# Reordering the opening of a Perceiver kernel: key rows in rounds, zeros moved, key and centre loads in another order

## The chip, the cores and the metric

The kernel runs on one core of a Trainium2 chip. The metric is the device time of one execution in microseconds (us); lower is better. A core has the engines PE (TensorE, matrix products), DVE (VectorE), ACT (ScalarE) and POOL (GpSimd), each with its own in-order stream of instructions, and SP (SyncE), whose stream here holds nearly all DMA issues, also in order. Engines wait for each other through semaphores.

## The reference

The whole computation is a Perceiver block of three residual parts on `x` (16 batches x 32 channels x 512 points):

```
x = x + xattn(ctx, layernorm(x), ...)    # graph features: what this change touches
x = x + attn(layernorm(x), ...)          # a Mamba-2 style scan
x = x + ffn(layernorm(x), ...)           # low-rank SwiGLU feed-forward
```

What matters is how the first part begins. Three channels of the context are taken as coordinates of the 512 points of each batch. They are quantized to 10 bits, four keys are made of them (two Morton, two Hilbert), and the points are sorted by each key:

```
keys = [morton(q), morton(qt), hilbert(q), hilbert(qt)]      # qt: x and y exchanged
inds = [window(argsort(k)) for k in keys]                    # 10 neighbours in sorted order
```

Then two graph layers follow. Each takes for every point and each of the four orders the 10 neighbours' features minus the point's own (the centre), does a small attention over the 10, a linear map and a 1x1 convolution, an instance norm, a leaky ReLU and a maximum over the neighbours. The third convolution joins the layers' outputs.

## The kernel before, in words

Four batches of 32 channels fill the 128 partitions: a "group". Four groups by two layers make eight stages, run in an order written out by hand in `graph_part`: `order = [(0, 0), (1, 0), (0, 1), ...]`. A stage has 43 blocks of 12 points. A software pipeline runs over all 8 x 43 blocks: in each step `scores`, `greatest`, `expo`, `sums`, `shares`, `turn`, `mapped`, `outputs` and `reduce` work on blocks up to four apart, and `differences` (POOL, L756 to L767) makes neighbour minus centre six blocks ahead (`LEAD`). After every third block, `differences` also issues four DMAs that copy its tile `DD` into the block-diagonal tile `DX` (L777). The other parts of `DX` have to be zero, and the scores (L809, PE) read `DX`.

The sort is done by counting. `compare` (L536) puts one product on PE that gives, for 128 points against all 512, the differences of their keys, and one ACT instruction (L537, `sgn`) that adds up their signs: this is the rank. A key is cut into bf16 rows in DRAM (`own` and `others`), and `load_keys` (L530, L531) brings the rows of one batch and one method by two DMAs to `kl` and `kr`, of which there are two sets. `rank_step` does one comparison per call, in order. The first 64 (`FIRST`) are batches 0 to 3 by methods 0 and 1 (eight each, `HALF`), then batches 0 to 3 by methods 2 and 3, the Hilbert keys.

`node_orders` makes the keys on DVE, in a generator that is stepped by hand. Its helper `rows` transposes a key on PE (L278) and splits it into bf16 rows: copy a part (L287; on ACT for the Morton key, on DVE for the Hilbert key), subtract it on PE (L289), copy the next part. Then it stores the rows (L293, L294). Before, all of the Hilbert key's `rows` stand between comparisons 24 and 25 in PE's order. After comparison 31 ACT writes zeros into the three `DX` tiles (L593).

`prep` prepares a stage, one piece per step. For the first stage it runs ahead of the loop, one `rank_step` after each piece. For layer 0 it does a layer norm (through ACT at L71 and L73), stores the features to DRAM (`dC`, L631), transposes them (`pf` L635, `FT` L637 on ACT) and splits them. Then, for each of the group's four batches: one-hot rows from the ranks (`oh`, DVE, L720), a product with the features on PE (`place`, L689, `pp`) that puts them in sorted order, a copy by ACT (`so`, L696, two buffers), a store to DRAM (`dS`, L700) and, three ticks later, four loads in another layout (`fs`, L706). The centre features come from `dC` by 16 loads (`crep`, L667). When all is there, DVE copies the last column (L738), and `differences` may begin.

`prep` queues stores and loads in a list `later` of delays, counted down by `tick`. Before, the 16 centre loads are one entry of that list: with delay 18 in the first stage, with delay 1 (at once) in the others. In the first stage they are issued behind the first batch's `fs` loads, and the 8 key loads of batch 4 follow them on SP, ahead of the store of the second batch.

Of the kernel before, what the change touches and what calls it, by code (L numbers as in the profile page):

```python
# [8 lines left out]
F32 = mybir.dt.float32  # L9
# [9 lines left out]
P = 128  # L19
# [4 lines left out]
M = 4  # L24
# [163 lines left out]
def node_orders(nc, pool, tmp, ps, X, idx, id32, nid, own, others):  # L188
# [81 lines left out]
    def rows(keys, j, copy):  # L270

        R = 2 * B
        at = slice(R * j, R * j + R)
        made = []
        for nm, src in zip("hl", keys):
            pr = ps.tile([R, D], F32, tag="pr", name=f"pr{nm}{j}", bufs=2)
            for c in range(4):
                nc.tensor.matmul(  # L278
                    pr[:, c * P:(c + 1) * P], lhsT=src[:, c].rearrange("p m b -> p (m b)"), rhs=id32,
                    is_transpose=True, start=(c == 0), stop=True, skip_group_check=True,  # L280
                )
            made.append((pr, pool.tile([R, 3, D], BF16, name=f"r{nm}{j}")))
        for k in range(3):
            for (pr, t), n, r0 in zip(made, (2, 3), (0, 4)):
                if k >= n:
                    continue
                copy(t[:, k], pr)  # L287
                if k < n - 1:
                    nc.tensor.matmul(  # L289
                        pr, lhsT=nid[:R, :R], rhs=t[:, k], start=False, stop=True, skip_group_check=True  # L290
                    )
                    continue
                nc.sync.dma_start(out=others[at, r0:r0 + n], in_=t[:, :n])  # L293
                nc.sync.dma_start(out=own[at, r0 + n:r0 + 2 * n], in_=t[:, :n])  # L294
# [3 lines left out]
    key = pool.tile([P, 2, N], I32, name="key0")  # L298
# [4 lines left out]
    for j in range(2):  # L303
        nc.vector.scalar_tensor_tensor(
            key[:, j], S[:, j], 2, key[:, j], ALU.logical_shift_left, ALU.bitwise_or
        )
    rows(parts(key.rearrange("p j n -> p (j n)"), 0), 0, nc.scalar.copy)
    yield

    H = [pool.tile([P, 2, N], I32, name=f"H{i}") for i in range(3)]  # L310
# [4 lines left out]
    flat = [h.rearrange("p a n -> p (a n)") for h in H]  # L315
# [39 lines left out]
    for s in (1, 2, 4, 8):  # L355
        t = new("y")
# [11 lines left out]
    nc.vector.scalar_tensor_tensor(key, XX[:, 0], 2, key, ALU.logical_shift_left, ALU.bitwise_or)  # L368
    keys = parts(key, 1)
    yield  # L370
    rows(keys, 1, nc.vector.tensor_copy)


def graph_part(nc, tc, cx, I, dram, id32, ones, xt, F0, layernorm_steps, rstd_steps, scan_input):
# [172 lines left out]
    def rank_step(tile_of):  # L547

        n = ranked[0]
        if n == 4 * M * B:  # L550
            return
        ranked[0] += 1
        if n < FIRST:
            half, k = divmod(n, HALF)
            b, c, m = half % 4, k // 2, 2 * (half // 4) + k % 2
        else:
            b, k = divmod(n, 4 * M)
            c, m = divmod(k, M)
        if n == 0:
            load_keys(0, (0, 1))  # L560
        compare(tile_of(n), b, c, m)
        if n < FIRST:
            if k == 1 and half < 7:
                load_keys((half + 1) % 4, (0, 1) if half < 3 else (2, 3))
            elif k == 1:
                load_keys(4, range(M))
        elif k == 4 and b + 1 < B:
            load_keys(b + 1, range(M))

# [12 lines left out]
    def first_tile(n):  # L582
        return kps.tile([P, D], F32, tag="kd", name=f"kd{n}", bufs=3)

    for n in range(3 * HALF + 1):
        rank_step(first_tile)
    for _ in orders:
        pass
    while ranked[0] < 4 * HALF:
        rank_step(first_tile)  # L590
    for t in DX:
        flat = t.rearrange("p h b q -> p (h b q)").bitcast(F32)
        nc.scalar.mul(flat, ones[:, 0:1].to_broadcast([P, flat.shape[-1]]), 0.0)  # L593


    id30 = gc.tile([P, QB], F32, name="id30")
# [22 lines left out]
    def later_tile(n):  # L619
        return ps_1.tile([P, D], F32, tag="misc", bufs=2, name=f"kd{n}")  # L620

    def prep(g, layer, delay=1):


        L, co, npair, WA, WC, HB = layers[layer]
        key = f"{L}_{g}"
        src = F1[g] if layer else F0[:, g]
        if layer == 0:
            yield from layernorm_steps(sm, src, xt[:, g], f"g{g}")
        dC = dram.tile([P, D], F32, name=f"dC{key}")  # L630
        nc.sync.dma_start(out=dC, in_=src)  # L631

        pf = ps_1.tile([P, 4, P], F32, tag="misc", bufs=2, name=f"pf{key}")
        for c in range(4):
            nc.tensor.transpose(pf[:, c], src[:, c * P:(c + 1) * P], id32)  # L635
        FT = wk.tile([P, 4, P], F32, tag="FT", name=f"FT{key}", bufs=1)
        nc.scalar.copy(FT, pf)  # L637
        yield

        F3 = [wk.tile([P, 4, P], BF16, tag=f"F3_{k}", name=f"F3_{k}{key}", bufs=1) for k in range(3)]  # L640
        for k in range(3):
            nc.vector.tensor_copy(F3[k], FT)
            if k < 2:
                nc.vector.tensor_tensor(FT, FT, F3[k], ALU.subtract)
                yield

        c16 = wk.tile([P, D], F16, tag="c16", name=f"c16{key}", bufs=1)
        nc.vector.tensor_copy(c16, src)
        yield
        c32 = wk.tile([P, D], F32, tag="c32", name=f"c32{key}", bufs=1)  # L650
        nc.vector.tensor_copy(c32, c16)
        yield
        hc = wk.tile([P, npair, D], F32, tag="hc", name=f"hc{key}")
        for pr in range(npair):
            ph = ps_1.tile([P, D], F32, tag="misc", bufs=2, name=f"ph{key}_{pr}")
            nc.tensor.matmul(ph, lhsT=WC[:, pr], rhs=c32, start=True, stop=True)
            nc.scalar.activation(hc[:, pr], ph, AF.Identity, bias=HB)
            yield

        crep = big.tile([P, 4, D], F32, tag="crep", name=f"crep{key}", bufs=2)  # L660
        later = []

        def copies():
            for b in range(4):
                for m in range(M):
                    r = 32 * b + 8 * m
                    nc.sync.dma_start(  # L667
                        out=crep[r:r + 8], in_=dC[32 * b:32 * b + 32].rearrange("(h c) n -> c h n", h=4)
                    )

        later.append([delay, copies])

        def tick():
            for t in list(later):
                t[0] -= 1
                if t[0] <= 0:
                    later.remove(t)
                    t[1]()

        yield  # L680

        fs = big.tile([P, 4, D + 4], F32, tag="fs", name=f"fs{key}", bufs=2)
        pend = []

        def place():
            b, c, ohs, pp = pend.pop()
            for m, oh in ohs:
                for k in range(3):
                    nc.tensor.matmul(  # L689
                        pp[32 * m:32 * m + 32, :], lhsT=F3[k][:, c, 32 * b:32 * b + 32], rhs=oh,  # L690
                        start=(c == 0 and k == 0), stop=(c == 3 and k == 2),
                    )
            if c < 3:
                return
            so = wk.tile([P, D], F32, tag="so", name=f"so{key}_{b}", bufs=2)
            nc.scalar.copy(so, pp)  # L696
            dS = dram.tile([P, D], F32, name=f"dS{key}_{b}")

            def store():
                nc.sync.dma_start(out=dS, in_=so)  # L700
                later.append([3, spread])

            def spread():
                for m in range(M):
                    r = 32 * b + 8 * m
                    nc.sync.dma_start(  # L706
                        out=fs[r:r + 8, :, :D], in_=dS[32 * m:32 * m + 32].rearrange("(h c) n -> c h n", h=4)
                    )

            later.append([2, store])  # L710

        for b in range(4):
            while ranked[0] < ranks_of(4 * g + b):
                yield False
            pp = None
            for c in range(4):
                ohs = []
                for m in range(M):
                    oh = wk.tile([P, D], BF16, tag="oh", name=f"oh{key}_{b}_{m}_{c}", bufs=8)
                    nc.vector.tensor_scalar(  # L720
                        oh, it2, rank[:, c, m, 4 * g + b:4 * g + b + 1], None, ALU.is_equal
                    )
                    ohs.append((m, oh))
                    if m == 1:
                        tick()
                        yield
                if pend:
                    place()
                if c == 0:
                    pp = ps_1.tile([P, D], F32, tag="pp", name=f"pp{key}_{b}")  # L730
                pend.append((b, c, ohs, pp))
                tick()
                yield
        place()
        while later:
            tick()
            yield
        nc.vector.tensor_copy(fs[:, :, D:], fs[:, :, D - 1:D].to_broadcast([P, 4, 4]))  # L738
        made[key] = (fs, crep, hc)
# [214 lines left out]
    made = {}  # L954
    order = [(0, 0), (1, 0), (0, 1), (1, 1), (2, 0), (3, 0), (2, 1), (3, 1)]
    keys = [f"{layers[layer][0]}_{g}" for g, layer in order]
    first = prep(*order[0], 18)
    next(first)
    for _ in first:
        if ranked[0] < FIRST:  # L960
            rank_step(early_tile)
    for gi in range(LEAD):
        differences(0, gi)

# [435 lines left out]
```

## Time and profile before

| what | us |
|---|---|
| median of 3 runs | 2449.3 (2441.37 to 2454.86) |
| the profiled execution | 2442.78 |
| its span, first to last instruction | 2440.9 |
| opening, up to the third batch's `so` copy | 98.62 |
| from there to the first scores of the loop (L809) | 30.36 |
| block loop of the eight stages, from there to about 1400 | 1271 |
| scan and feed-forward parts, the rest | about 1040 |

The profile is of one execution. A row of the timeline gives start, busy time, engine (SPq is the DMA-issuing queue of SP), line, operation, output<-inputs, shape, count, and in brackets the idle time of that engine just before with what ended it. Lines of the waits give the total, the number and the longest. A row of a window gives, for a stretch, each engine's busy time with its number of instructions, the granted PE clock as a share of full speed, the busy share of the DMA engines and GB/s. Line numbers are those of the kernel before.

### The profile page before, as it was taken

To read this page: it belongs to the slowest core of one execution; us is meant where nothing else is said; L and a number is where in the kernel's file an instruction comes from. 1 tells how busy PE (TensorE), PEld (TensorE's weight loads), DVE (VectorE), ACT (ScalarE), POOL (GpSimd) and SP (SyncE) were. 2 spreads that over 40 slices of the span, in tenths; PEclk is the share of its full clock that TensorE was granted. 3 is DMA by queue.
4 is the path that set the end of the run, shared out by engine and by line. 5 is a ranking of instruction groups with operands and counts; after the bars stand their busy time and mean duration, and the time that the engine had idled before them with its cause. 6 is when DMAs were issued, how large, how long until landed. Compare 5 with 4: busy or idle time off the path is not lost. (4 is left out here: it accounts for less than half of the span.)

```text
span 2440.9 us, 88578 instructions
## 1 busy us (share of the span) xinstructions
PE 2135.6 (87%) x39025; PEld 1247.9 (51%) x39146; DVE 1739.5 (71%) x3718; ACT 1098.7 (45%) x2023; POOL 830.9 (34%) x897
## 2 busy tenths in 40 slices
PE   5479677999899677879998879999999999999979
PEld 2145455667667454566777634444444444444422
DVE  8379798888899889988999866653554626455643
ACT  5567556666665334454555322332333424333331
POOL 2056556445446556564655400020211202021200
PEclk9889999999999899999999889999999999999989
DMA  2232232221122233322211222213122131310000
GB/s 48 60 65 65 57 74 61 58 59 44 43 62 59 52 73 65 72 52 67 58 34 40 63 73 75 75 31 95 52 61 65 39 86 31 87 57 22 26 35 17
DMA packets 121624, 137.98 MB, mean 57 GB/s; under 512 B 18398, under 2 KB 79506, under 8 KB 121154
## 3 DMA queue, kind: packets, MB, share of 16 engines
q1 hardware_dynamic: 121240, 132.32, 21.6%
q8 instruction: 307, 5.03, 0.9%
q14 instruction: 77, 0.63, 0.1%
HBM read 77.02 MB, written 12.85 MB: 37 GB/s over the span
## 5 line engine op out<-in xcount | busy, mean ns | idle before, releaser
L846 POOL TENSOR_TENSOR EN<-e,rz 128x480 f32<-128x480 f32 x344 | 342.3, 995 | 561.4 <-DVE rz L844 424.1
L871 PE MATMUL u<-WA,DD 128*32 128x128 bf16 (+1 forms) x16512 | 421.6, 251 | 51.1 <-issue 34.2
L871 PEld LDWEIGHTS <-DD 128*32 128x32 f16 x16512 | 341.1, 99 | 69.8 <-issue 66.0
L876 ACT COPY us<-u 128x512 f32<-128x512 f32 x516 | 301.9, 586 | 151.9 <-PE u L871 133.6
L831 ACT ACTIVATE e<-s,smc 128x480 f32<-128x480 f32 x344 | 227.2, 660 | 287.0 <-PE s L826 253.4
L767 POOL TENSOR_TENSOR DD<-fs,crep 128x480 f16<-128x480 f32 (+2 forms) x344 | 349.5, 1017 | 0.0
L890 PE MATMUL h<-e,us 128*32 128x30 f32 (+1 forms) x11008 | 286.1, 211 | 58.2 <-DVE e L852 23.9
L890 PEld LDWEIGHTS h<-e,us 128*32 128x32 f32 (+1 forms) x11008 | 253.2, 127 | 143.8 <-issue 53.5
L1098 DVE SCALAR_TENSOR_TENSOR cyh<-ppch,t_conv_w,cyh 128x496 f32<-128x496 f32 (+2 forms) x192 | 137.5, 716 | 221.6 <-ACT cyh L1093 217.6
L818 DVE TENSOR_REDUCE c<-s 128x16 bf16<-128x480 f32 x344 | 219.6, 638 | 73.2 <-PE s L809 70.4
L1247 PE MATMUL po<-wo,gs 128*128 128x512 f32 x512 | 240.5, 605 | 10.5 <-DVE xt L1250 10.3
L1174 POOL TENSOR_TENSOR da<-lei,dA 128x512 f32<-128x512 f32 x32 | 40.5, 1268 | 612.0 <-PE pl L1179 577.6
L1086 PE MATMUL ppch<-hT,winch 128*128 128x512 f32 x512 | 232.2, 593 | 0.0
L1086 PE MATMUL ppg<-hT,wing 128*128 128x512 f32 x512 | 231.9, 593 | 0.0
L852 DVE STREAM_TRANSPOSE e<-EN 128x512 f32<-128x512 f32 x344 | 224.5, 653 | 0.6 <-POOL EN L846 0.6
L838 DVE TENSOR_REDUCE z<-e 128x16 f32<-128x480 f32 x344 | 219.4, 638 | 0.0
L537 ACT ACTIVATE sgn<-kd 128x512 bf16<-128x512 f32 x256 | 153.0, 598 | 73.9 <-PE kd L536 44.9
L809 PE MATMUL s<-DX,DD 128*32 128x120 f16 x5504 | 144.5, 224 | 33.8 <-DMA DX<-DD 27.4
L809 PEld LDWEIGHTS <-DD 128*32 128x32 f16 x5504 | 82.3, 97 | 178.3 <-issue 133.6
L720 DVE TENSOR_SCALAR oh<-it,rank 128x512 bf16<-128x512 f16 x512 | 166.9, 386 | 7.8 <-PE pp L689 7.8
L1086 PEld LDWEIGHTS ppch<-hT,winch 128*128 128x128 f32 x512 | 93.6, 190 | 122.7 <-issue 122.4
L826 PE MATMUL s<-c,idb 128*128 128x480 bf16 x344 | 131.5, 382 | 28.4 <-DVE c L818 26.8
(323 smaller groups left out, 2746.0 us busy)
## 6 DMA issues: line engine op xcount, KB each, us to landing
DX<-DD SPq DMA_DIRECT2D x456, 90.0 KB
wo<-in_out_proj SPq DMA_DIRECT2D x64, 256.0 KB
wing<-in_in_proj SPq DMA_DIRECT2D x64, 256.0 KB
winch<-in_in_proj SPq DMA_DIRECT2D x64, 256.0 KB
dS<-so SPq DMA_DIRECT2D x32, 256.0 KB
fs<-dS SPq DMA_DIRECT2D x128, 64.0 KB
crep<-dC SPq DMA_DIRECT2D x128, 64.0 KB
wincB<-in_in_proj SPq DMA_DIRECT2D x8, 256.0 KB
```

What stands on the lines that cost most here:

```text
L767: nc.gpsimd.tensor_tensor(d[:, :, m0 - n0:n1 - n0], win, crep[:, :, m0:n1].unsqueeze(3).to_broadcast([P, 4, n1 - m0, K]), ALU.subtract,)
L809: nc.tensor.matmul(s[rh, j * 4 * QB:(j + 1) * 4 * QB].rearrange("p (b q) -> p b q", b=4), lhsT=d[:, h, c0:c0 + 32], rhs=dx[:, h, :, c0:c0 ...
L818: nc.vector.tensor_reduce(c, live["s", at, gi].rearrange("p (i q) -> p i q", q=QB), AX.X, ALU.max, negate=True)
L831: nc.scalar.activation(e, s.rearrange("p (i q) -> p i q", q=QB), AF.Exp, scale=smc)
L838: nc.vector.tensor_reduce(z, e, AX.X, ALU.add)
L846: nc.gpsimd.tensor_tensor(en[:, :, :QB], e, rz.unsqueeze(2).to_broadcast([P, NI, QB]), ALU.mult)
L852: nc.vector.transpose(e.rearrange("p i q -> p (i q)"), en.rearrange("p i q -> p (i q)"))
L871: nc.tensor.matmul(u[rh, jj], lhsT=d[:, h, c0:c0 + 32], rhs=WA[k][:, h].rearrange("p b o -> p (b o)"), start=(jj == 0 and k == 0), stop=(k ...
L876: nc.scalar.copy(us[:, j - jj:j + 1], u)
L890: nc.tensor.matmul(h[r:r + co, pr, q0:q0 + QB], lhsT=us[:, j, b * co:(b + 1) * co], rhs=e[:, 4 * j + b, :QB], start=True, stop=True,)
L1086: nc.tensor.matmul(pp, lhsT=w[:, k], rhs=hT[:, k], start=(k == 0), stop=(k == 3))
L1247: nc.tensor.matmul(po, lhsT=gs[:, i, q * P:(q + 1) * P], rhs=wo[i], start=(i == 0), stop=(i == TG - 1))
```

## The change

It adds and removes no instruction; it reorders.

1. `rows` yields before each of its three rounds, and the Hilbert key's rounds are called with two comparisons between them. 24 comparisons, not 25, stand ahead of the Hilbert transposes.
2. The zeros of `DX` are written after the first stage's `prep`, that is behind the copy of the last `so`, and ahead of the first `differences`.
3. `rank_step` no longer loads the keys of batch 0, methods 2 and 3, and of batch 4 by itself. The first are loaded after comparison 31, the second after the first stage's `prep`, behind its last `fs` loads on SP.
4. The centre loads: in the first stage all 16 are issued before the first one-hot rows (in SP's order behind the keys of batch 1, methods 2 and 3, ahead of those of batch 2). In the seven other stages, four are issued behind each of the four `dS` stores, ahead of that batch's `fs` loads.

```diff
         for k in range(3):
+            yield
             for (pr, t), n, r0 in zip(made, (2, 3), (0, 4)):
...
-    rows(keys, 1, nc.vector.tensor_copy)
+    yield from rows(keys, 1, nc.vector.tensor_copy)
...
-            if k == 1 and half < 7:
+            if k == 1 and half != 3 and half < 7:
                 load_keys((half + 1) % 4, (0, 1) if half < 3 else (2, 3))
-            elif k == 1:
-                load_keys(4, range(M))
...
-    for n in range(3 * HALF + 1):
+    for n in range(3 * HALF):
         rank_step(first_tile)
     for _ in orders:
-        pass
+        for _ in range(2):
+            rank_step(first_tile)
     while ranked[0] < 4 * HALF:
         rank_step(first_tile)
-    for t in DX:
-        flat = t.rearrange("p h b q -> p (h b q)").bitcast(F32)
-        nc.scalar.mul(flat, ones[:, 0:1].to_broadcast([P, flat.shape[-1]]), 0.0)
+    load_keys(0, (2, 3))
...
-    def prep(g, layer, delay=1):
+    def prep(g, layer, early=False):
...
-        def copies():
+        def centre(b):
+            for m in range(M):
+                r = 32 * b + 8 * m
+                nc.sync.dma_start(
+                    out=crep[r:r + 8], in_=dC[32 * b:32 * b + 32].rearrange("(h c) n -> c h n", h=4)
+                )
+
+        if early:
             for b in range(4):
...
-        later.append([delay, copies])
+                centre(b)
...
             def store():
                 nc.sync.dma_start(out=dS, in_=so)
+
+                if not early:
+                    centre(b)
                 later.append([3, spread])
...
-    first = prep(*order[0], 18)
+    first = prep(*order[0], early=True)
     next(first)
     for _ in first:
         if ranked[0] < FIRST:
             rank_step(early_tile)
+    load_keys(4, range(M))
+    for t in DX:
+        flat = t.rearrange("p h b q -> p (h b q)").bitcast(F32)
+        nc.scalar.mul(flat, ones[:, 0:1].to_broadcast([P, flat.shape[-1]]), 0.0)
     for gi in range(LEAD):
         differences(0, gi)
```

More of the change, by code (lines that the diff above doesn't have):

```diff
@@ L306, in node_orders @@
         )
-    rows(parts(key.rearrange("p j n -> p (j n)"), 0), 0, nc.scalar.copy)
+    for _ in rows(parts(key.rearrange("p j n -> p (j n)"), 0), 0, nc.scalar.copy):
+        pass
     yield
@@ L661, in prep @@
         later = []
-        def copies():
-            for b in range(4):
[L665 to L669, printed above, removed]
-        later.append([delay, copies])
+        def centre(b):
[5 more added lines that the diff above has]
+        if early:
+            for b in range(4):
+                centre(b)
         def tick():
```

## The prediction

> **What bounds the kernel now.** I read the engine rows first: PE 87%, DVE 71%, no engine full, so a gain has to be looked for by stage. The chain of waits only follows the last 100 us (the feed-forward part), which the change does not touch. So I cut the time by stage: the stretch 98.62 to 128.98, between the opening and the block loop, is nearly empty (PE 4.21 of 30.36 us busy, DVE 3.36, ACT 1.17). The timeline of ACT shows two more holes in the opening:
>
> ```profile
> 49.46 0.19 ACT L537 ACTIVATION_READ_ACCUMULATOR sgn<-kd 128x1 f32 x1
> 56.94 0.60 ACT L537 ACTIVATE sgn<-kd 128x512 bf16<-128x512 f32 x1 [7.29 <-PE kd L536]
> ...
> 61.84 7.57 ACT L593 ACTIVATE DX<-ones 128x2880 f32<-128x2880 f32 x3
> 69.32 0.19 ACT L71 ACTIVATE rss_g<-rst_g 128x1 f32<-128x1 f32 x1
> ...
> 72.36 0.58 ACT L637 COPY FT<-pf 128x512 f32<-128x512 f32 x1 [2.62 <-PE pf L635]
> ```
>
> See: 7.29 us in which ACT waits for a comparison, then 7.57 us of zeros ahead of the Ln (L71) that the first layer norm needs. From 72.36 to 98.62 ACT does a comparison every 0.72 us almost without a break: it is the bound there, and all behind it moves with it. Then the SP queue (start, issuing time):
>
> ```profile
> 87.74 0.35 SPq L700 DMA_DIRECT2D dS<-so  x1
> 89.77 1.31 SPq L706 DMA_DIRECT2D fs<-dS  x4
> 91.12 9.49 SPq L667 DMA_DIRECT2D crep<-dC  x16
> 101.09 0.28 SPq L530 DMA_DIRECT2D kr<-others  x1
> ...
> 105.46 0.34 SPq L700 DMA_DIRECT2D dS<-so  x1
> 107.52 1.30 SPq L706 DMA_DIRECT2D fs<-dS  x4
> 108.92 0.34 SPq L700 DMA_DIRECT2D dS<-so  x1
> 112.46 1.30 SPq L706 DMA_DIRECT2D fs<-dS  x4
> 113.86 0.34 SPq L700 DMA_DIRECT2D dS<-so  x1
> 117.52 1.30 SPq L706 DMA_DIRECT2D fs<-dS  x4
> 122.16 0.17 DVE L738 COPY fs<-fs 128x16 f32<-128x16 f32 x1 [19.87 <-DMA fs<-dS]
> 128.98 0.36 PEld L809 LDWEIGHTS <-DD 128*32 128x32 f16 x16 [25.80 <-POOL DD L767]
> ```
>
> See: the second batch's `so` was copied at 93.23, but its store issues only at 105.46, behind 16 centre loads and 8 key loads. The last `so` (PE ready near 103.2) waits for that store's buffer until 107.58, and the loop starts 6.8 us after L738.
>
> **The change part by part.** Sums are made against the profiled execution: 2442.78 us (span 2440.9), 6.5 us under the median of 2449.3.
>
> *Rounds.* By the listed instruction order, comparison 24 moves behind the eight Hilbert transposes, and pairs 24/25, 26/27, 28/29 stand between the rounds; no instruction is added. ACT ends comparison 23 at 48.9 (0.7 earlier). The transposes still wait for DVE's key (PE at 51.71) and end at 53.5; comparison 24 follows, and ACT starts it 0.70 us later (as 56.24 to 56.94 before): 54.2. Eight at 0.72 are 5.8 us, so 60.0 if the rounds don't starve ACT; its end now is 61.95. Price: the third rows (L287 on DVE, 0.68 us each) have to wait for PE pairs, so the last row is about 0.6 us later (57.6). The stores to `others`/`own` and the key loads of batch 0 behind them go with it, landing near 62.9, when PE wants them near 63. Bounds: 0 (every pair waits for a row) to -1.9; I take -1.8.
>
> *Zeros.* 3 x 2.52 = 7.57 us leave the path ahead of L71: -7.57. They come back behind the last `so` copy. What hides them: after that copy ACT has nothing until 130.23 in the loop, and the DMA that reads them is POOL's first DX copy (124.86), over 9 us after the copy in the new order. Without that cover they would cost the 7.57 again.
>
> So the FT copy comes at about 63.0 instead of 72.36: -9.3.
>
> *Centre loads of the first stage.* All 16 move ahead of the keys of batch 2, methods 2 and 3. dC issues near 62.0, lands about 2.0 later (as dS, 87.74 to 89.77), then the 16 loads take 7.2 to 9.6 us (the eight such blocks in the trace): 64 to 72.6. Queued behind them: four key loads, by the gaps at 101.09 to 103.4 about 2.4 us, landing near 77. Comparison 48 wants them on PE near 76.6. Added wait 0 to 2 us, on ACT's bound; I take 0.5. The keys of batch 3, then dS0, come after that in time. `so` of the third batch: 98.62 - 9.3 + 0.5 = 89.8.
>
> *Keys of batch 4 last.* Their 8 loads (101.09 to 105.4) no longer stand before the stores; they issue behind the last fs loads, near 98.5 to 103, and are wanted by the loop's first comparison near 110: hidden.
>
> *The stores.* Now dS1 issues as soon as `so` is there, so the last `so` waits only for PE: 103.2 + 0.1 - 98.62 = 4.7 us after the third, plus 0.58: ready at 95.1. dS3 then takes 2.03 to 3.66 us to its fs loads; the long ones stood right behind other fs loads, here these end a microsecond before: 2.5. From the fs issue to L738 is 4.64 (117.52 to 122.16). L738: 95.1 + 2.5 + 4.64 = 102.3 against 122.16, about -19.9 in all.
>
> *What is late next:* the loop needs POOL's differences, 6.8 us after L738, unchanged, so its start moves by -19.9 too. The 0.5 clock there stays:
>
> ```profile
> 103.50:106.00 2.50, 0.00 (x0) 0.00 (x0) 0.00 (x0) 0.00 (x0) 0.00 (x0) 1.00 0.20 50
> 106.00:108.50 2.50, 0.00 (x0) 0.00 (x0) 0.00 (x0) 0.58 (x1) 0.00 (x0) 0.92 0.31 114
> 108.50:111.00 2.50, 0.00 (x0) 0.00 (x0) 0.00 (x0) 0.00 (x0) 0.00 (x0) 0.50 0.65 161
> 138.50:141.00 2.50, 2.50 (x81) 1.34 (x70) 2.43 (x6) 2.22 (x6) 0.36 (x1) 0.93 0.02 7
> ```
>
> The seventh column is the granted clock: it fell some 4.5 us after PE's last work and came back near 138.7, 9.7 us after the restart. But PE was also idle from 60.4 to 71.2, and there the clock fell only near 77. The Trainium skill (TensorE: Matmul & The Clock Gate, Part 1) says that one idle window of about 3.4 us brings the half clock, and as much busy time the full one. By the rule the new gap of some 14 us (95 to 109) still ends cold: 0. By the row around 77, a shorter gap can start warm: up to half of the 7.1 us that PE was busy at 0.50, -3.5. I take 0, since the 14 us are nearer to the gap that went cold.
>
> *Centre loads of the other seven stages.* The block of 16 (7.2 to 9.6 us of SP) becomes 4 behind each of the four stores. Gain: loads behind the block come earlier, but PE's waits on DX copies were only 1.9 us outside the opening (27.4 on the page, 25.5 of them at 129): 0 to -1.9. Loss: four loads now stand between a store and its fs loads. The Trainium skill (DMA: Bandwidth & Descriptors, Queues, rings and completion order) says that each DMA engine consumes its ring in order, which speaks against this place: the last fs loads queue behind 256 KB, 1.6 us at the 161 GB/s of the row above, or 2.4 us as a quarter of a 16-block. But the fs loads wait 2.0 to 3.7 us for the store anyway, and most of it hides there. It matters only where DVE sits waiting:
>
> ```profile
> DVE fs L738 <- DMA fs<-dS: 21.8, 4, 11.5
> ```
>
> Of these the largest, 11.46 at 265.89, has fs loads directly behind the store; the others (5.53, 4.41) have their fs loads 6 to 8 us later. Bounds -1.9 to +5; I take +0.5 in sum.
>
> **Sum:** -1.8 - 7.6 + 0.5 - 11.0 (the stores) + 0.5 = -19.4. On the profile 2442.8 becomes 2423.4; on the median 2449.3 - 19.4 = 2429.9.
>
> **The rivals.**
> (A) Starved comparisons. The first stage's centre loads take 9.6 us, keys come 2 us late, the pairs of the rounds win nothing, dS3 takes 3.66: +1.5 + 1.8 + 1.2, so about -15: 2434. For: SP was this stage's bottleneck. Against: its loads now have 4 us fewer neighbours.
> (B) The gain is given back at stage ends: L738 late by 2.4 us at all seven, +16.8, net -3: 2446. For: ring order, and L738 stops DVE. Against: three of seven show a large wait, and the store's latency covers the loads.
> (C) Slower. Centre loads spread over 28 stores push the DX copies behind them by about 2 us each, and scores (L809), in order on PE, stop the loop: 28 x 2 = 56, less 19.9: +36, 2485. It decides once a DX copy lands later than its slack: made four blocks of about 3.3 us ahead, and needing about 6 us of them to issue and land, it has some 5 to 7 us. Against: today's blocks of 7 to 9.6 us cost only 1.9 in all.
> (D) The change doesn't do what it says: the listed order shows the zeros, rounds, keys and centre loads where the text puts them, so only "four at a time" can be idle. Included in A.
>
> **How the numbers follow.** Main case 0.70 (-17 to -22, 2427 to 2432, run-to-run some 5 us either way as the runs of before spread 2441 to 2455), A 0.09, B 0.13, C 0.08. Half a per cent (12 us) is about what a measurement of this kernel can tell from no change. Faster: main 0.69 and A 0.07 = 0.76; same: main 0.01, A 0.02, B 0.13 = 0.16; slower: C 0.08. Range 2420 to 2441: it holds the main case with its noise and A, and leaves out most of B and C.
>
> **What would show it.** Right: in the profile after, ACT's hole near 49 to 57 ends by 54.5; FT is copied near 63; dS stores each issue within 0.5 us of their `so`; L738 near 102 with a wait under 8 us; first L809 near 109; zeros between 95 and 103 with ACT idle behind; and the loop from first L809 to the end as long as before (2312 us) within 3. Wrong: comparison 48 waiting for keys more than 2 us (A); L738 waits in the loop summing to over 30 us (B); PE s L809 waiting for DX in the loop over 10 us (C); or the loop longer by what the opening won.

## The result, and the profile after

| what | before, us | after, us |
|---|---|---|
| median of 11 runs each | 2450.31 (2439.64 to 2454.86) | 2435.03 (2428.99 to 2442.76) |
| ratio, 95% interval | | 0.9944 [0.9926, 0.9962] |
| profiled execution, its span | 2442.78, 2440.9 | 2429.63, 2427.9 |
| FT copy | 72.36 | 63.32 |
| first column copy (L738, now L741) | 122.16 | 103.61 |
| first scores (L809, now L812) | 129.01 | 110.45 |
| first scores to the end of the span | 2311.9 | 2317.5 |

The changed kernel is faster by 13.7 us by the ratio (9.3 to 18.1; the medians themselves lie 15.3 apart). The opening won 18.5 us up to the first scores; in the profiled executions 5.6 of them are gone again at the end.

ACT in the timeline of the kernel after (start, busy, engine, line, operation, output<-input, and the idle time before it in brackets):

```profile
54.08 0.60 ACT L539 ACTIVATE sgn<-kd 128x512 bf16<-128x512 f32 x1 [5.12 <-PE kd L538]
...
60.18 0.19 ACT L539 ACTIVATION_READ_ACCUMULATOR sgn<-kd 128x1 f32 x1
60.27 0.19 ACT L71 ACTIVATE rss_g<-rst_g 128x1 f32<-128x1 f32 x1
63.32 0.59 ACT L636 COPY FT<-pf 128x512 f32<-128x512 f32 x1 [2.62 <-PE pf L634]
...
94.87 0.59 ACT L696 COPY so<-pp 128x512 f32<-128x512 f32 x1 [3.98 <-PE pp L689]
95.35 7.59 ACT L968 ACTIVATE DX<-ones 128x2880 f32<-128x2880 f32 x3
111.68 0.60 ACT L539 ACTIVATE sgn<-kd 128x512 bf16<-128x512 f32 x1 [8.74 <-PE kd L538]
```

The first hole shrank from 7.29 to 5.12 us. L71 follows directly behind the last comparison, and the zeros now run in a stretch behind which ACT has 8.74 us of nothing to do. The last `so` waits for PE's product (`pp`), no longer for a store.

SP, then DVE and PE, in the timeline of after:

```profile
64.47 8.38 SPq L665 DMA_DIRECT2D crep<-dC  x16
...
79.41 0.35 SPq L700 DMA_DIRECT2D dS<-so  x1
81.44 1.30 SPq L709 DMA_DIRECT2D fs<-dS  x4
85.52 0.34 SPq L700 DMA_DIRECT2D dS<-so  x1
87.84 1.30 SPq L709 DMA_DIRECT2D fs<-dS  x4
...
95.48 0.34 SPq L700 DMA_DIRECT2D dS<-so  x1
98.59 1.30 SPq L709 DMA_DIRECT2D fs<-dS  x4
99.98 0.28 SPq L532 DMA_DIRECT2D kr<-others  x1
103.61 0.17 DVE L741 COPY fs<-fs 128x16 f32<-128x16 f32 x1 [9.64 <-DMA kr<-others]
110.42 0.37 PEld L812 LDWEIGHTS <-DD 128*32 128x32 f16 x16 [15.57 <-POOL DD L770]
```

Each store issues about 0.6 us behind the start of its `so` copy, which takes 0.6. The column copy comes 8.1 us behind the last store (before: 8.3), and the scores 6.8 us behind the column copy, as before: the end of the chain is the same, it only starts 18.4 us earlier.

Windows of after around the start of the loop (the stretch, its length, PE, PEld, DVE, ACT, POOL busy, granted PE clock, DMA share, GB/s):

```profile
95.00:97.50 2.50, 0.14 (x1) 0.00 (x0) 0.00 (x0) 2.50 (x2) 0.00 (x0) 1.00 0.64 177
97.50:100.00 2.50, 0.00 (x0) 0.00 (x0) 0.00 (x0) 2.50 (x2) 0.00 (x0) 0.67 0.15 47
...
117.50:120.00 2.50, 2.50 (x69) 1.38 (x68) 1.68 (x4) 1.78 (x6) 0.00 (x0) 0.73 0.10 23
120.00:122.50 2.50, 2.11 (x69) 1.14 (x68) 2.43 (x6) 2.50 (x8) 0.41 (x1) 1.00 0.03 7
```

PE's last product ends near 95.1, the clock is at half by 100, and it comes back about 8 us behind the restart at 110.4. The shorter gap still ends cold, so the term of 0 for the clock holds.

One line went the wrong way. From the waits between 130 and 1420 us of after (total, number, longest):

```profile
DVE fs L741 <- DMA fs<-dS: 23.8, 5, 14.5
```

Before it was 21.8, and 11.5 for the longest.

### The profile page after: what moved, and what is told of

Same layout as the page of the kernel before. It is cut to its first block, busy times and chain, and to the rows that moved or that the text cites. A ratio compares the mean times of both kernels' runs of the same rounds, so it can differ in the third digit from the quotient of the medians.

```text
span 2427.9 us, 88565 instructions
## 1 busy us (share of the span) xinstructions
PE 2137.0 (88%) x39024; PEld 1249.5 (51%) x39146; DVE 1739.6 (72%) x3718; ACT 1099.8 (45%) x2023; POOL 831.7 (34%) x897
## 5 line engine op out<-in xcount | busy, mean ns | idle before, releaser
L812 PEld LDWEIGHTS <-DD 128*32 128x32 f16 x5504 | 82.1, 97 | 164.1 <-issue 127.7
L812 PE MATMUL s<-DX,DD 128*32 128x120 f16 x5504 | 144.0, 224 | 20.3 <-DMA DX<-DD 17.0
```

The source lines that it names most:

```text
L812: nc.tensor.matmul(s[rh, j * 4 * QB:(j + 1) * 4 * QB].rearrange("p (b q) -> p b q", b=4), lhsT=d[:, h, c0:c0 + 32], rhs=dx[:, h, :, c0:c0 ...
```

## The experiments

Every kernel was timed against the kernel before on its own chip; a difference in us is (ratio - 1) times that chip's median of before. Diffs are against the changed kernel unless said otherwise. The four opening kernels ran on one chip; the loop kernels on two others, called first and second in their table.

### The change again, and a control for single profiles

No edit. `after_again`:

> The changed kernel once more, beside the three that follow. Theory 1 (ring order: in stages 2 to 8 the four centre loads stand in front of the last fs loads, and those land some 2.4 us later where DVE waits for them): the DVE copy of the last column waits near 14.5 us at the first stage end and 2 to 3 us at the fourth (before: 11.5 and 0.3), as in the first profile of the changed kernel; the loop from the first scores to the end is near 2317 us again. Theory 2 (the 5.5 us by which the loop was longer in that profile is run-to-run scatter of the loop): other waits, and a loop anywhere between 2310 and 2320. Time 2430 to 2438 us, 0.5 to 0.7 per cent under before.

`after_third`:

> The changed kernel once more, beside the two others on the same chip. Both theories: ratio 0.993 to 0.996. If the opening and the loop add up, its difference to before equals block16's plus loop_only's within 3 us.

Measured: 0.9939 [0.9918, 0.996] and 0.9939 [0.9923, 0.9955]. In three measurements, the last two on different chips, the change is worth 13.7, 14.9 and 14.9 us. The profile of `after_again` shows one thing that the first did not (ACT timeline, comparisons of batch 2):

```profile
79.24 0.60 ACT L539 ACTIVATE sgn<-kd 128x512 bf16<-128x512 f32 x1 [1.03 <-PE kd L538]
82.85 0.60 ACT L539 ACTIVATE sgn<-kd 128x512 bf16<-128x512 f32 x1 [0.87 <-PE kd L538]
```

Here the keys behind the 16 centre loads came late; with two smaller waits it is 2.4 us, and the first scores came at 113.28 instead of 110.45. In `after_third` they came at 109.68.

`before_again`, no edit of the kernel before:

> The kernel before, a second profiled execution, as a control for single profiles: if the stretch from first scores to the end differs from 2311.9 us by 3 us or more, a single profile's stretch can't carry a difference of a few microseconds, and only the timed runs and the waits can; if it is within 1 us, the longer stretches of the other profiles (2316 to 2324) are effects of their edits.

Measured: one time, 2447.03. First scores at 127.52 (129.01 in the first profile), and 2317.7 us from there to the end, not 2311.9. So for the same kernel the stretch from the first scores to the end differs by 5.8 us between two profiled executions. The 5.6 us by which this stretch looked longer in after cannot be read from one pair of profiles; in `after_again` and `after_third` it is 2320.4 and 2318.9. The waits at the stage ends are steadier: DVE's waits for the column copy in the loop (all six or fewer that the timeline shows) sum to 22.6 and 22.4 us in the two profiles of before, to 26.6, 24.9 and 26.9 in the three of after.

### The opening, one part undone at a time

`zeros_back`: the zeros of DX back behind comparison 31.

```
+    for t in DX:
+        nc.scalar.mul(flat, ones[...], 0.0)      # ahead of the layer norm
 ...
-    for t in DX: ...                             # behind the first stage's prep
```

> The changed kernel with the zeros of DX written by ACT after comparison 31 again; rounds, keys and centre loads as changed. The prediction's term: they stand ahead of the layer norm again, so the FT copy comes 7.6 us later than in the changed kernel (63.3 to 70.9) and the first scores too (110.5 to 118): 2437 to 2443 us. Rival: the later stage of the opening has slack of its own (SP waits for centre loads, which would now have been done), and less than 6 us comes through to the first scores.

`no_rounds`: all Hilbert rounds in one piece behind comparison 24.

```
-    for n in range(3 * HALF):
+    for n in range(3 * HALF + 1):
         rank_step(first_tile)
     for _ in orders:
-        for _ in range(2):
-            rank_step(first_tile)
+        pass
```

> The changed kernel with the Hilbert rows made at one stretch again, 25 comparisons ahead of them. The prediction's term: the last of the first 32 comparisons ends 1.6 to 1.9 us later than in the changed kernel, and the first scores too: 2432 to 2438 us. Rival: the rows and their stores, 0.6 us earlier without the pairs in between, set the pace instead, and there is no difference at the first scores.

`stores_old`: in the first stage the centre loads at delay 18, and the keys of batch 4 ahead of the stores, both as before.

```
+            elif k == 1 and half == 7:
+                load_keys(4, range(M))
 ...
-        if early:
-            for b in range(4):
-                centre(b)
+        if early:
+            later.append([18, copies])
 ...
-    load_keys(4, range(M))
```

> The changed kernel with the first stage's 16 centre loads behind the first batch's fs loads again and batch 4's keys behind them, ahead of the second store; zeros and rounds as changed. The prediction's term: the last so waits for the second store again, and the column copy comes 9 to 11 us later than in the changed kernel (103.6 to 113 to 115), the first scores too: 2440 to 2447 us. Rival: with ACT 9 us earlier the block on SP starts earlier too and is half hidden; then 5 us or less.

`keys_later`: the keys of batch 4 only behind the first DX copies.

```
-    load_keys(4, range(M))
     for t in DX: ...
     for gi in range(LEAD):
         differences(0, gi)
+    load_keys(4, range(M))
```

> The changed kernel with batch 4's keys issued behind the first DX copies instead of right behind the last fs loads. If the keys' loads slow the last fs loads down (the trace of the changed kernel puts the end of the DVE wait down to a key load): issue to column copy 4.6 us or less instead of 5.0, and 0.4 us or more earlier scores. If not: 5.0 us again, and the first comparison of the loop may wait for its keys, up to 2 us more.

| kernel | ratio | FT copy | column copy | first scores |
|---|---|---|---|---|
| after (profile) | see above | 63.32 | 103.61 | 110.45 |
| zeros_back | 0.997 [0.9952, 0.9988] | 70.44 | 112.43 | 119.28 |
| no_rounds | 0.9952 [0.9938, 0.9966] | 64.85 | 105.21 | 112.05 |
| stores_old | 0.9988 [0.9975, 1.0001] | 63.33 | 112.57 | 119.41 |
| keys_later | 0.9951 [0.9928, 0.9975] | 63.34 | 103.47 | 110.32 |

ACT in the timeline of `zeros_back`, then of `no_rounds`:

```profile
59.92 7.57 ACT L595 ACTIVATE DX<-ones 128x2880 f32<-128x2880 f32 x3
70.44 0.59 ACT L639 COPY FT<-pf 128x512 f32<-128x512 f32 x1 [2.62 <-PE pf L637]
...
85.56 0.60 ACT L539 ACTIVATE sgn<-kd 128x512 bf16<-128x512 f32 x1 [1.08 <-PE kd L538]
```

```profile
56.90 0.60 ACT L539 ACTIVATE sgn<-kd 128x512 bf16<-128x512 f32 x1 [7.22 <-PE kd L538]
64.85 0.59 ACT L635 COPY FT<-pf 128x512 f32<-128x512 f32 x1 [2.62 <-PE pf L633]
```

The zeros put back cost 7.1 us at the FT copy and 8.8 at the first scores; the rest is waits for keys of the kind shown for `after_again`, one of 1.08 us in the last row. The rounds put back bring the 7.22 us hole again and cost 1.5 at the FT copy, 1.6 at the first scores.

The timeline of `stores_old` (SP, ACT, DVE):

```profile
82.79 8.56 SPq L667 DMA_DIRECT2D crep<-dC  x16
...
95.31 0.34 SPq L705 DMA_DIRECT2D dS<-so  x1
97.43 0.59 ACT L701 COPY so<-pp 128x512 f32<-128x512 f32 x1 [6.54 <-DMA dS<-so]
...
112.57 0.17 DVE L746 COPY fs<-fs 128x16 f32<-128x16 f32 x1 [18.59 <-DMA fs<-dS]
```

With the block back in front of the second store, that store issues at 95.31 instead of 85.52. The last `so` is 2.6 us later than in after, but the column copy 9.0: the three stores and their loads form a chain on SP (each store to its fs loads 2.0 to 3.9 us), which ends long after the last `so`. Undone one by one, the parts cost 8.8, 1.6 and 9.0 us at the first scores: 19.4 together, against 18.5 of all at once. They add up within what single profiles can tell (the first scores of the changed kernel lie 3.6 us apart between three profiles).

The timed runs say the same more coarsely. On this chip `zeros_back`, `no_rounds` and `stores_old` are 7.3, 11.7 and 2.9 us faster than the kernel before, and `keys_later`, whose opening is that of the changed kernel, 12.0. Against `keys_later` the zeros cost 4.6, the rounds 0.2 and the stores 9.0 us, each with some 7 us either way: by time alone only the stores' part is clear.

`keys_later` moves nothing at the first scores (110.32). The profile of after names `kr<-others` as what the first column copy waited for; taking those loads away from there leaves the time from the fs issue to the copy at 4.90 us (5.02 in after). So the wait was for the fs loads, and the name is that of a DMA which completed at about the same time: the trace has the last fs load of after complete at 103.54 and the key load at 103.73, and the copy starts at 103.61.

### The loop: centre loads four at a time

`block16`: as the changed kernel, but from the second stage on the 16 centre loads go in one block at once, as before.

```
-        if early:
-            for b in range(4):
-                centre(b)
+        def copies():
+            for b in range(4):
+                centre(b)
+        if early:
+            copies()
+        else:
+            later.append([1, copies])
 ...
                 nc.sync.dma_start(out=dS, in_=so)
-                if not early:
-                    centre(b)
```

> The changed kernel with the centre loads of stages 2 to 8 in one block of 16 again, at once after the store of dC; all else as changed. Theory 1: from the issue of the last fs loads to the DVE copy 4.9 us again at the first stage end (7.2 in the changed kernel), its wait near 11.5, and the loop 3 to 5 us shorter than in the changed kernel: 2427 to 2432 us. Theory 2: waits and time as in the changed kernel, within 1 us. Theory 3 (the spreading pays by letting DX copies through): the loop 2 us longer than in the changed kernel.

`block16_again`, the same kernel on another chip:

> The version with all changes but the spread loads in stages 2 to 8, once more on another chip. Theory (ring order costs what the first look showed): ratio 0.989 to 0.992, 6 to 11 us under the changed kernel. Rival (the first look was a favourable set of executions and the true cost is the 3.5 to 4 us of column-copy waits): ratio 0.992 to 0.9935, 3 to 4 us under the changed kernel.

`first_three`: no centre loads in front of a stage's last fs loads.

```
-                if not early:
+                if not early and b < 3:
                     centre(b)
+                    if b == 0:
+                        centre(3)
```

> The changed kernel with no centre loads in front of the last batch's fs loads in stages 2 to 8: batch 3's four go behind the first store, beside batch 0's. Theory 1: as for the block of 16, issue to copy 4.9 us and the loop 3 to 5 us shorter than in the changed kernel, 2427 to 2432 us, since only the last four loads are in the way. Theory 2: no difference from the changed kernel beyond 1 us in the waits. If the loss were from all 28 groups of four (DX copies pushed back), it would stay as in the changed kernel.

`twice`: the four centre loads behind each store issued twice (no other data).

```
                 if not early:
                     centre(b)
+                    centre(b)
```

> The changed kernel with the four centre loads behind each store in stages 2 to 8 issued twice (the same data again): double the suspected cost. Theory 1: the fs loads land another 2.4 us later at the stage ends where DVE waits: issue to copy near 9.5 us at the first and fourth stage end, the waits there near 17 and 5, and 5 to 8 us more in all than the changed kernel. Theory 2: no step of 2.4 us at those two ends; at most the added issue time of 1.3 us.

`loop_only`, the other way round: the kernel before, and only the centre loads of the seven later stages as in the changed kernel (diff against before).

```
+        if delay == 18:
             later.append([delay, copies])
 ...
                 nc.sync.dma_start(out=dS, in_=so)
+                if delay != 18:
+                    centre(b)
```

> The kernel before with one edit: in the seven later stages the centre loads go four behind each store, as in the changed kernel; the whole opening is that of before. Theory (ring order: the last fs loads of a stage land 2.3 to 2.8 us later where DVE waits for them): ratio about 1.002 to 1.004, 4 to 10 us slower; first scores unchanged near 129; the column copies at the first stage's end 7 to 7.7 us behind the fs issue instead of 4.9, the sum of their waits 26 to 27 us instead of 22.6. Rival (the prediction's term: hidden behind the store's latency, and what blocked blocks cost is regained): ratio 1.000 within 0.0015 (0 to 1 us). Rival (the difference seen between the block version and the changed kernel came from the early centre loads of the opening only): ratio 1.000 and fs issue to copy 4.9 us.

| chip | kernel | ratio | us against before | column copy at the first stage's end: wait, fs issue to copy |
|---|---|---|---|---|
| first | after_again | 0.9939 [0.9918, 0.996] | -14.9 | 13.86, 7.43 |
| first | block16 | 0.9896 [0.9874, 0.9918] | -25.5 | 11.30, 5.16 |
| first | first_three | 0.991 [0.9889, 0.993] | -22.0 | 11.44, 4.65 |
| first | twice | 1.004 [1.0028, 1.0053] | +9.8 | 18.60, 6.64 |
| second | after_third | 0.9939 [0.9923, 0.9955] | -14.9 | 13.78, 7.65 |
| second | block16_again | 0.9924 [0.9908, 0.9939] | -18.6 | 11.96, 4.74 |
| second | loop_only | 1.0027 [1.0016, 1.0039] | +6.6 | 13.39, 7.35 |

`loop_only` settles the sign: the spread loads alone make the kernel slower, by 3.9 to 9.5 us. `block16` agrees from the other side: 10.5 us under the changed kernel on one chip, 3.7 on the other, where the two intervals overlap and the smaller cost, the rival of `block16_again`, came out. `first_three` gets most of it back although it still spreads the loads over three stores. On the second chip `block16_again` and `loop_only` add up to -12.0 us against the -14.9 of `after_third`, just within the 3 us that were forecast. All point to about 7 us, with an uncertainty of some 3.

The profiles do not show this in the length of the loop. From the first scores to the end `block16` and `block16_again` take 2320.6 and 2321.2 us, no less than the changed kernel's 2317.5 to 2320.4, so the 3 to 5 us by which `block16` was to be shorter there were not seen; their profiled executions (2433.3 and 2433.1 us) are among the slowest of their six. The total rests on the timed runs, the place on single waits.

Where it happens, in the timelines of before, after, `block16`, `twice` and `loop_only`, DVE at the end of the first stage:

```profile
265.89 0.17 DVE L738 COPY fs<-fs 128x16 f32<-128x16 f32 x1 [11.46 <-DMA fs<-dS]
```
```profile
250.77 0.17 DVE L741 COPY fs<-fs 128x16 f32<-128x16 f32 x1 [14.52 <-DMA fs<-dS]
```
```profile
248.75 0.17 DVE L744 COPY fs<-fs 128x16 f32<-128x16 f32 x1 [11.30 <-DMA fs<-dS]
```
```profile
256.54 0.17 DVE L742 COPY fs<-fs 128x16 f32<-128x16 f32 x1 [18.60 <-DMA fs<-dS]
```
```profile
270.94 0.17 DVE L744 COPY fs<-fs 128x16 f32<-128x16 f32 x1 [13.39 <-DMA fs<-dS]
```

In the eight profiles with four loads per store this wait lies between 13.39 and 14.65 us, in the five with none before the last fs loads between 11.30 and 11.96: 2.5 us between the means, without overlap. At the end of the fourth stage the same shows in five of the eight (2.7 to 3.6 us against 0.3 to 1.2). (The profile names a DX copy as what ended those five waits, but in after the last fs load completes at 739.21 and the column copy starts at 739.29.) At the other five ends nothing shows.

Why: the issues on SP at that end, in after and in `block16`. The fs loads issue equally late in both, 2.2 and 2.0 us behind the store:

```profile
241.37 0.34 SPq L700 DMA_DIRECT2D dS<-so  x1
241.76 1.38 SPq L665 DMA_DIRECT2D crep<-dC  x4
243.60 1.30 SPq L709 DMA_DIRECT2D fs<-dS  x4
```
```profile
241.57 0.34 SPq L705 DMA_DIRECT2D dS<-so  x1
243.59 1.30 SPq L712 DMA_DIRECT2D fs<-dS  x4
```

The windows from that store to the column copy (columns as above), first of after, then of `block16`:

```profile
241.40:242.90 1.50, 0.00 (x0) 0.00 (x0) 0.00 (x0) 0.00 (x0) 0.00 (x0) 0.61 0.52 180
242.90:244.40 1.50, 0.00 (x0) 0.00 (x0) 0.00 (x0) 0.00 (x0) 0.00 (x0) 0.50 0.53 122
244.40:245.90 1.50, 0.00 (x0) 0.00 (x0) 0.00 (x0) 0.00 (x0) 0.00 (x0) 0.50 0.54 79
245.90:247.40 1.50, 0.00 (x0) 0.00 (x0) 0.00 (x0) 0.00 (x0) 0.00 (x0) 0.50 0.56 76
247.40:248.90 1.50, 0.00 (x0) 0.00 (x0) 0.00 (x0) 0.00 (x0) 0.00 (x0) 0.50 0.56 79
```
```profile
241.60:243.10 1.50, 0.00 (x0) 0.00 (x0) 0.00 (x0) 0.00 (x0) 0.00 (x0) 0.66 0.48 178
243.10:244.60 1.50, 0.00 (x0) 0.00 (x0) 0.00 (x0) 0.00 (x0) 0.00 (x0) 0.50 0.08 15
244.60:246.10 1.50, 0.00 (x0) 0.00 (x0) 0.00 (x0) 0.00 (x0) 0.00 (x0) 0.50 0.47 109
246.10:247.60 1.50, 0.00 (x0) 0.00 (x0) 0.00 (x0) 0.00 (x0) 0.00 (x0) 0.50 0.34 55
```

In `block16` there is a real hole behind the store (0.08 of DMA, 15 GB/s), as the prediction assumed. After's centre loads fill it and run on beyond it. They and the fs loads run at 76 to 79 GB/s, with about half of the DMA engines' time busy, whereas the store ran at about 180. An estimate from these rows: 256 KB of centre loads at 79 GB/s are 3.3 us; the hole takes 1 to 1.4 of them, and about 2 are left in front of the fs loads, near the 2.5 measured.

The trace also holds the steps in which each DMA's semaphore counts up; no view prints them, but they show the order. In after the four centre loads are complete at 244.97, 245.82, 246.66 and 247.49, the four fs loads at 248.34, 249.19, 250.02 and 250.59. In `block16` the fs loads, issued at the same time, are complete at 246.37, 247.21, 248.01 and 248.57. So the loads finish one behind the other in the order of their issue, some 0.85 us each, and the whole row of fs loads moves back by 2.0 us. If the two groups had shared the DMA engines evenly, they would have ended together. The same order stands in `after_again`, `after_third`, `no_rounds` and `loop_only`, where the first fs load completes 0.91 to 0.97 us behind the last centre load.

With eight loads (`twice`) the fs loads themselves issue only 6.5 us behind the store (2.0 in `block16`), because SP takes 6.06 us to issue them.

`twice` also shows when the prediction's slower rival wakes up. Its waits between 130 and 1420 us:

```profile
SPq L665 <- DMA crep<-dC: 87.7, 97, 3.0
...
PE s L813 <- DMA DX<-DD: 13.7, 8, 3.4
```

PE's waits for DX rise from 1.7 us in after to 13.7, and SP waits for its own outstanding loads. It is 24.7 us slower than the changed kernel of the same chip, where 5 to 8 were forecast: SP's waits were not foreseen. The column copy's waits explain 13 to 15 of it (39.6 in sum against 26.6 in the first profile of after and 24.9 in `after_again`).

`block16` is the best version of all: 18.6 to 25.5 us under the kernel before, on two chips.

## Why the prediction was right

It gave 2430 (2420 to 2441) with -19.4 us; 2435.03 and -13.7 were measured. Faster held because the opening behaved as worked out; the distance between the two numbers is mostly one term of the loop. In part the range held by luck: -13.7 lies outside the main case (-17 to -22), near the -15 of rival A, for whose sake the range reached that far, but it was the loop that took the difference and not the starved comparisons of A.

- *Rounds*, -1.8: comparison 24 was foreseen at 54.2 and came at 54.08. Undone, they cost 1.6 at the first scores of one profile; by the timed runs this is too small to see. Right as far as the profile shows.
- *Zeros*, -7.6: FT was foreseen at 63.0 and came at 63.32; undone, 7.1 at that place. Right, and the cover that was named (ACT idle behind the last `so`) is there.
- *Keys behind the centre loads*, +0.5: nothing in the first profile, 2.4 us in the second. The bound of 0 to 2 held in the first profile and not in the second; the price scatters between executions. This is rival A's mechanism, and it takes part in some executions.
- *Stores*, -11.0: foreseen were the last `so` at 95.1, dS to fs 2.5, L738 at 102.3. They were 94.87, 3.11 and 103.61. The step on the store failed: it counted the fs loads of the third batch as over a microsecond before (their issue was), but they take some 5 us from issue to use, and the last store, 1.67 us behind their issue (95.48 - 93.81), still met them: the trace has them complete up to 98.21, and of the store's 16 parts eight at 97.37 to 97.48, the other eight only at 98.02 to 98.57. The copy came 5.0 instead of 4.64 behind the issue. Undoing this part alone costs 9.0. Mechanism right, size 1 to 2 us too large.
- *What is late next*: the 6.8 us of POOL up to the scores stayed (110.45 - 103.61), and the clock stayed cold. Right. (The case named against it, a clock still full behind PE's idle stretch from 60.4 to 71.2, is shown only from 74.0 on, where the clock record of that trace begins.) The opening as a whole: the three profiles with the old opening have first scores at 127.52, 129.01 and 131.84, the eight with all parts of the new one (`keys_later` among them) at 110.45 on average, so -19.0 against the predicted -19.9.
- *Centre loads of the other seven stages*, +0.5: this is the term that was mis-sized. It costs about 7 us (+6.6 in `loop_only`). The step that failed is "most of it hides there". The prediction priced 256 KB by a row of 161 GB/s, in which a store ran; loads of this shape run at 79, so they need 3.3 us, twice the 1.6, and the hole behind the store hides only 1 to 1.4. The Trainium skill's rule on rings consumed in order (DMA: Bandwidth & Descriptors, Queues, rings and completion order) was the side to believe: the runs show 2.5 us at this place, close to the 2.4 that the prediction worked out as the quarter of a block and then took to be hidden. The trace agrees with the rule: the fs loads complete behind all four centre loads, one by one in the order of issue (248.34 behind 247.49), and not mixed with them.
- *Rival B* (2.4 us at all seven ends, +16.8) had the right price and too many places: one end always, one in most executions. Its mark, column waits over 30 us in sum, was not reached (26.6; 29.4 at most in the other profiles with four loads per store). *Rival C* shows only with twice the loads. *D* fell: the change does what it says.
- Two marks of "right" failed. The column copy waited 9.64 us, not under 8. The loop was 5.6 us longer, not within 3; but this mark was badly chosen, since two profiles of the kernel before differ by 5.8 in it.

What stays open: of the 7 us the column copies' waits show about 3.7 (26.4 on average over the eight profiles with four loads per store, 22.7 over the four with blocks of 16). In `loop_only` by itself they show even less: 26 to 27 us were forecast for their sum and 23.2 came, 0.7 over before: the 1.9 us more at the first end stand beside smaller waits at the others. Where the rest lies was not found; the stretch from the first scores to the end is too unsteady to cut further.

## What to carry to other kernels

Ask of each transfer that is moved what queue it stands in and who sits waiting at the end of it: 16 loads in one block far ahead of a deadline cost little here (PE waited 1.8 us for DX copies in `block16`), while four in front of the last, awaited loads cost 2.5 us where those followed at once and an engine sat waiting. Price a transfer by the rate of a row with the same kind of transfer, not by the highest rate nearby. In an opening where one chain sets the end, parts of it can be costed singly and added (19.4 against 18.5, where profiles scatter by 3.6); in a pipelined loop take the timed runs and particular waits, and profile the old kernel twice before a few microseconds of one profile are believed.

## What the hardware showed that was not expected

- Loads of 64 KB from DRAM in this layout ran at 76 to 79 GB/s with the DMA share at 0.54 to 0.56, right behind a 256 KB store that moved at 180 GB/s with a share of 0.52. About the same busy share, less than half of the rate. The semaphore of such a load counts up in eight steps as its data lands, that of the store in sixteen. That fits loads which keep eight of the sixteen DMA engines busy and leave the others idle, but the trace does not name the engines.
- The time from a 256 KB store to the issue of the loads that wait for it went up from one to the next in after's opening (2.03, 2.32, 2.90, 3.11 us) while the distance to the issue of the loads before it went down (none, 4.1, 3.1, 1.7 us); in `stores_old`, at 1.4 us, it was 3.65 and 3.85. A store behind loads still in flight is slower by up to 1.8 us. Half of the last store of after lands as early as a quiet store, 2.0 us behind its issue, and half only when the loads ahead of it are complete (98.21), up to 98.57. No run tried this by itself.
- The opening of the kernel before scatters by 4.3 us between three executions of the same instructions, at the key loads behind its block of 16; that of the changed one by 3.6 between three.
